# Attention layer: the next image's patches fetched in eight pieces over eight steps, and a third buffer for the result

## The chip, the cores and the metric

The kernel runs on one core of a Trainium2 chip. A core has five instruction queues that run beside each other: TensorE (PE in the profile, with PEld for the loading of its weights), VectorE (DVE), ScalarE (ACT), GpSimd (POOL) and SyncE (SP). They meet only through semaphores. Transfers are carried by 16 DMA engines; an engine's queue issues a transfer and goes on to its next instruction, and whoever needs the data waits for the transfer's semaphore. In this kernel nearly all transfers are issued by SP, one after the other in the order in which they stand in SP's program.

The metric is the device time of one execution in microseconds, as the median of several runs. All arithmetic is in fp32.

## The reference, cut to what matters

The program is four layers on an image batch `x` of shape (8, 16, 256, 256): 8 images, 16 channels, 256 x 256 pixels. Each layer normalises its input by groups of two channels and adds its result to `x`.

```
x = x + L0(gn(x))     # convolution with routing by agreement
x = x + L1(gn(x))     # spline convolution
x = x + L2(gn(x))     # attention over patches: the layer that is changed
x = x + L3(gn(x))     # circular 3x3 convolution
```

The attention layer treats every channel of every image by itself. The 256 x 256 pixels are cut into 16 x 16 patches of 16 x 16 pixels; that is a matrix of 256 patches by 256 pixels.

```
t = (patches + emb).transpose(0, 1, 3, 2)
Q, K, V = t @ Wq.T + bq, t @ Wk.T + bk, t @ Wv.T + bv
A   = sigmoid(einsum('bcph,bcpg->bchg', K, Q) / 16)
out = einsum('bcph,bchg->bcpg', V, A)          # 256 x 256 per image and channel
```

So there are 8 x 16 = 128 independent problems of one size.

## The kernel before

The layers run one after the other. Layer 2, the attention (`layer2`, lines 1432 to 1632), walks through the list `todo`: image by image, and in each image channel by channel, which gives 128 steps. Its instructions stand on every engine in the order in which the Python code issues them: the loop is inside a manual schedule, and no planner moves anything. (The planner with due times at the top of the file belongs to layer 0.)

One step for image b and channel c does the following, in this order:

- In four of 16 steps (c = 2, 6, 10, 14) SP issues the load `res2` (`rows`, line 1480): the layer's input for four channels, in the layout in which it is added to the result. It is 1024 KB, in two buffers that take turns, and the step in which it is issued is two or three steps before its first use.
- At c = 3, `patches` (line 1470) fetches all patches of the next image, in two transfers, one for each half of its 256 patches. Each is issued by `patch` (line 1427): 128 partitions, each with 16 channels x 8 runs of 32 floats (128 B), which is 16,384 runs and 2048 KB. They go to one of two places that take turns by the image's number: image 1, 3, 5, 7 to `pt1`, image 2, 4, 6 to `pt0` (the same memory that layer 3 uses later for its image 0). Image 0 has been fetched at the end of layer 1, by the same function in eight pieces of 512 KB.
- `prepare` for the next step (line 1492): DVE normalises the next channel's patches out of `pt` into `t` (L1496), and POOL adds the embedding and forms four sums (L1500 to L1506).
- `product`, `values`, `rest` (lines 1511 to 1554): PE's matmuls for Q, K and V, and DVE's additions that collect them (L1523 to L1526, L1537 to L1539); ACT turns V into `vt` (L1554).
- `output` for the *previous* step (line 1573): PE multiplies V with A into the PSUM tile `po` (L1579). DVE adds `res2` and writes the result `y2` (L1584), takes its statistics (L1591, L1592); POOL copies the wrapped edge columns (L1593, L1594), and SP issues the store of `y2` to the array `x3` (L1595). One `y2` is 128 partitions x 2064 B, 258 KB.
- `score` (line 1556): PE's product K x Q, and ACT's sigmoid into `a` (L1571), which the next step's `output` reads.

Three orders matter for the change.

- On DVE: L1584 stands behind the current step's L1539 and ahead of the next step's L1496, L1523 and so on. If L1584 waits, all of DVE waits.
- On SP: a step's issues are `res2` if any, then the patches if any, then the store of the previous step's `y2`. That store waits for DVE's L1584 and POOL's copies, so the patches of a step go out right behind the store before.
- Buffers: `y2` has two, so L1584 of one step has to wait until the store of the result two steps earlier has landed. `u2`, `qk` and `a` have one, `t`, `ds`, `vt` and `po` two.

Each transfer on SP also waits until the eighth transfer before it has landed, since eight semaphores take turns.

In the last image (its c from 4 to 12) SP also loads the first two images for layer 3; in that image no patches are fetched, since there is no next image.

Of the kernel before, what the change touches and what calls it, by code (L numbers as in the profile page):

```python
# [10 lines left out]
F32 = mybir.dt.float32  # L11
# [6 lines left out]
B, C, H, W = 8, 16, 256, 256  # L18
P = 128
WP = W + 2  # L20
# [272 lines left out]
class _Net:  # L293
# [1138 lines left out]
    def layer2(self, images=range(B), channels=range(C)):  # L1432
# [3 lines left out]
        with ExitStack() as st:  # L1436
# [3 lines left out]
            mid = st.enter_context(tc.tile_pool(name="l2_mid", bufs=2))  # L1440
# [26 lines left out]

                return get

            def patches(b):  # L1470

                pt = self.pt[b % 2]
                for half in range(2):
                    self.patch(b, half, 0, C)
                return pt

            def rows(b, c):

                res = load.tile([P, 4, 16, 2, 16], F32, name="res2")
                nc.sync.dma_start(  # L1480
                    out=res.rearrange("p c n k j -> p c (n k j)"),
                    in_=self.x2[b][c : c + 4].rearrange("c r h n k j -> (r h) c (n k j)"),
                )
                return res

            pts, ress = {images[0]: self.pt[images[0] % 2]}, {(images[0], 0): first}
# [5 lines left out]
            def prepare(b, c):  # L1492

                bc = final["bc"] if b == images[-1] else self.bc2
                t = self.tpool.tile([P, 2, 8, 32], F32, name="t")
                nc.vector.tensor_scalar(  # L1496
                    t, pts[b][:, :, c], bc[:, 0, b, c : c + 1], bc[:, 1, b, c : c + 1], ALU.subtract, ALU.mult
                )
                t = ts[b, c] = t.rearrange("p h r f -> p h (r f)")
                nc.gpsimd.tensor_tensor(t, t, self.emb0 if c == 0 else emb[:, :, c], ALU.add)  # L1500
                d = sums[b, c] = self.tpool.tile([P, 4, P], F32, name="ds")
                a11, a12, a21, a22 = t[:, 0, :P], t[:, 1, :P], t[:, 0, P:], t[:, 1, P:]
                nc.gpsimd.tensor_tensor(d[:, 0], a21, a22, ALU.add)
                nc.gpsimd.tensor_tensor(d[:, 1], d[:, 0], a11, ALU.subtract)
                nc.gpsimd.tensor_tensor(d[:, 2], a11, a21, ALU.subtract)
                nc.gpsimd.tensor_tensor(d[:, 3], a12, d[:, 1], ALU.subtract)  # L1506
# [4 lines left out]
            def product(b, c):  # L1511

                t, d = ts[b, c], sums[b, c]
                ps = part[b, c] = [psum.tile([P, 256], F32, name=f"pq{i}") for i in range(4)]
                mm(ps[0], t[:, 0, :P], q0, True, True)
                mm(ps[1], d[:, 1], wt[:, 1], True, True)
                mm(ps[2], d[:, 2], wt[:, 2], True, True)
                mm(ps[3], d[:, 0], wt[:, 0], True, True)
                u = mid.tile([P, 2, 256], F32, name="u2", bufs=1)
                qk = qks[b, c] = mid.tile([P, 2, 512], F32, name="qk", bufs=1)  # L1520
                both = bqk.rearrange("p (i n) -> p i n", i=2)
                last = qk[:, 1, 256:]
                nc.vector.tensor_tensor(u, ps[0].unsqueeze(1).to_broadcast([P, 2, 256]), both, ALU.add)  # L1523
                nc.vector.tensor_tensor(u, ps[1].unsqueeze(1).to_broadcast([P, 2, 256]), u, ALU.add)
                nc.vector.tensor_tensor(last, ps[2], u[:, 1], ALU.add)
                nc.vector.tensor_tensor(last, ps[3], last, ALU.add)  # L1526
                part[b, c].append(u)

            def rest(b, c):

                t, d = ts[b, c], sums.pop((b, c))
                *ps, u = part.pop((b, c))
                qk = qks[b, c]
                mm(ps[0], t[:, 1, :P], q1, False, True)
                mm(ps[2], t[:, 1, P:], wt[:, 3], False, True)
                mm(ps[3], d[:, 3], k1, False, True)
                nc.vector.tensor_tensor(qk[:, 0, :256], ps[0], bqk[:, :256], ALU.add)  # L1537
                nc.vector.tensor_tensor(qk[:, 1, :256], ps[2], u[:, 0], ALU.add)
                nc.vector.tensor_tensor(qk[:, 0, 256:], ps[3], u[:, 1], ALU.add)  # L1539

            def values(b, c):

                t = ts[b, c]
                pv = psum.tile([P, 2, 256], F32, name="pv")
                vt = vts[b, c] = mid.tile([P, 2, 2, 8, 2, 8], F32, name="vt")
                for k in range(2):
                    for n in range(2):
                        nc.tensor.matmul(  # L1548
                            pv[:, k], wv[:, n, k * P : (k + 1) * P], t[:, n, :], start=n == 0, stop=n == 1
                        )  # L1550
                for k in range(2):
                    src = pv[:, k].rearrange("p (r i o s) -> p o s i r", r=8, i=2, o=2)
                    for o in range(2):
                        nc.scalar.activation(vt[:, k, o], src[:, o], AF.Identity, bias=bv[:, k : k + 1])  # L1554
# [18 lines left out]
            def output(b, c):  # L1573

                res, vt, a = ress[b, c // 4], vts.pop((b, c)), avs.pop((b, c))
                po = psum.tile([P, 2, 256], F32, name="po", tag="po", bufs=2)
                for o in range(2):
                    for k in range(2):
                        nc.tensor.matmul(  # L1579
                            po[:, o], vt[:, k, o].rearrange("p s i r -> p (s i r)"), a[:, k, :], start=k == 0, stop=k == 1  # L1580
                        )
                y = mid.tile([P, 2, WP], F32, name="y2", bufs=2)
                inner = y[:, :, 1 : 1 + W]
                nc.vector.tensor_tensor(  # L1584
                    inner.rearrange("p o (n j) -> p o n j", j=16),
                    po.rearrange("p o (n j) -> p o n j", j=16),
                    res[:, c % 4].rearrange("p n k j -> p k n j"),
                    ALU.add,
                )
                i = b * C + c  # L1590
                nc.vector.bn_stats(stats[0][:, i, :], inner)  # L1591
                nc.vector.bn_aggr(stats[1][:, :, i], stats[0][:, i])  # L1592
                nc.gpsimd.tensor_copy(y[:, :, 0:1], y[:, :, W : W + 1])  # L1593
                nc.gpsimd.tensor_copy(y[:, :, WP - 1 : WP], y[:, :, 1:2])  # L1594
                nc.sync.dma_start(  # L1595
                    out=self.x3[b][:, c].rearrange("r h k w -> r h (k w)"), in_=y.rearrange("p k w -> p (k w)")
                )

            def step(steps):
                if steps:  # L1600
                    steps.pop(0)[2]()
                while steps and steps[0][0] != "PE":
                    steps.pop(0)[2]()

            with tc.manual_schedule():
                prepare(*todo[0])
                for i, (b, c) in enumerate(todo):
                    n = images.index(b)
                    after = images[n + 1] if n + 1 < len(images) else None
                    if c in (2, 6, 10):  # L1610
                        ress[b, c // 4 + 1] = rows(b, c + 2)
                    if c == 3 and after is not None:
                        pts[after] = patches(after)
                    if c == 14 and after is not None:
                        ress[after, 0] = rows(after, 0)
                    if c == 2 and n == 1:
                        final["bc"], late = self.stats2_steps(self.small, "g2b", bank)
                    if c == 1 and after is None:
                        self.bc3, after3 = self.stats3_steps(self.small, "g3a", bank)
                    if 4 <= c < 13 and after is None:  # L1620
                        self.first3(images[:2], c - 4)
                    if i + 1 < len(todo):
                        prepare(*todo[i + 1])
                    product(b, c)
                    values(b, c)
                    rest(b, c)
                    if i:
                        output(*todo[i - 1])
                    step(late)
                    step(after3)  # L1630
                    score(b, c)
                output(*todo[-1])
# [241 lines left out]
```

## Time and profile before

| | us |
|---|---|
| median of 3 runs | 6216.76 (6212.52 to 6217.24) |
| the profiled execution: its time | 6214.83 |
| the profiled execution: its span, first to last instruction | 6213.1 |
| PE busy in the span | 5875.4 (95%) |
| DVE busy | 5178.3 (83%) |
| POOL busy | 3821.4 (62%) |
| ACT busy | 3074.7 (49%) |
| first result of layer 2 (L1584) starts | 4886.89 |
| last result of layer 2 (L1584) starts | 5981.44 |

The profile is one execution, and every duration in this text is from it. "Busy" is time in which an engine executes; an engine's idle time is listed with whoever released it at its end. The granted clock is the share of PE's full clock that the chip's throttle gave in a stretch. A line number stands for the line of the kernel that issued the instruction. The DMA columns give the mean busy share of the 16 DMA engines and the bytes per second that they moved. For transfers that SP issues the profile has the length of the issue on SP, not the landing; it writes the transfers' sizes in KB of 1024 B, and lists the 14 large patch transfers of layer 2 with a wrong size of 0.1 KB, because their shape is set by a separate instruction (MOVE_SHAPE) ahead of them. The sizes above are counted from line 1427.

### The profile page before, as it was taken

How to read it: one execution, taken by the hardware profiler on the slowest of the kernel's cores; microseconds unless marked ns; L12 is line 12 of the kernel's file. 1: busy time of each engine (PE TensorE's matmuls, PEld its weight loads, DVE VectorE, ACT ScalarE, POOL GpSimd, SP SyncE). 2: the span in 40 equal slices, each digit the busy share in tenths (PEclk: the TensorE clock that was granted, in tenths of full speed). 3: DMA queues.
4: the chain of work that ended last, by engine and by line, in shares of the span. 5: the costliest groups of instructions: out<-in, count | busy, mean ns of one | idle time of the engine just before them, and what ended most of it. 6: DMA issues, size and time to landing. Idle time of an engine off the chain costs nothing.

```text
span 6213.1 us, 114828 instructions
## 1 busy us (share of the span) xinstructions
PE 5875.4 (95%) x45256; PEld 2923.1 (47%) x45256; DVE 5178.3 (83%) x6415; ACT 3074.7 (49%) x4858; POOL 3821.4 (62%) x3552
## 2 busy tenths in 40 slices
PE   2999999999999999999967999999999999999998
PEld 0344444444444444444423444444444688888863
DVE  5799999999999999999978999999999666666641
ACT  0444544454444444444427888888888222121221
POOL 0588888888888888888873334344443334333333
PEclk9999999999999999999978999999999999999999
DMA  7455555455555555555515555555557443444358
GB/s 287 120 138 127 142 142 135 126 145 139 134 130 145 136 133 134 143 138 130 133 45 183 175 176 177 176 173 176 177 176 184 136 84 94 84 98 99 91 179 268
DMA packets 408812, 902.32 MB, mean 145 GB/s; under 512 B 62034, under 2 KB 195762, under 8 KB 364882
## 3 DMA queue, kind: packets, MB, share of 16 engines
q1 hardware_dynamic: 364434, 831.69, 49.0%
q10 hardware_dynamic: 33984, 34.08, 1.8%
q0 software_dynamic: 9856, 29.20, 1.6%
q8 instruction: 359, 5.88, 0.4%
q14 instruction: 179, 1.47, 0.1%
HBM read 684.09 MB, written 210.77 MB: 144 GB/s over the span
## 4 chain that ended last, share of the span: by engine, by line
PE 56%; DVE 27%; issue 7%; DMA 4%; POOL 4%; ACT 2%; DVEq 0%; SPq 0%; POOLq 0%; ACTq 0%
PE rb L831 8%; PE cv L587 7%; DVE bases L1089 7%; PE pq L1509 6%; PE pl L733 6%; DVE e L1079 4%; PE cv L591 4%; PE cv L550 4%; PE po L1579 3%; PE p L1691 3%; PE psc L1563 3%; PE pv L1548 3%; DVE pr L723 2%; DVE a L1079 2%; DVE e L1058 2%
## 5 line engine op out<-in xcount | busy, mean ns | idle before, releaser
L1112 PE MATMUL ps<-bases,tw 128*32 128x512 f32 (+1 forms) x13824 | 1360.9, 545 | 16.2 <-POOL bases L1081 6.6
L851 POOL TENSOR_TENSOR dd<-dd 128x1024 f32<-128x1024 f32 x512 | 1212.7, 2369 | 70.8 <-DVE dd L842 65.5
L1081 POOL TENSOR_TENSOR bases<-e,a 128x1024 f32<-128x1024 f32 (+1 forms) x264 | 621.9, 2379 | 927.4 <-DVE e L1079 927.4
L723 DVE TENSOR_TENSOR pr<-v,fb 128x2048 f32<-128x2048 f32 (+1 forms) x512 | 1021.0, 2015 | 17.0 <-PE pl L733 12.5
L1112 PEld LDWEIGHTS ps<-bases,tw 128*32 128x32 f32 x13824 | 598.5, 109 | 800.1 <-issue 483.8
L842 DVE SCALAR_TENSOR_TENSOR dd<-rb,v 128x1024 f32<-128x1024 f32 x768 | 907.0, 1215 | 8.9 <-POOL dd L851 3.3
L851 POOL TENSOR_TENSOR s<-s,dd 128x512 f32<-128x512 f32 x512 | 648.0, 1276 | 15.1
L831 PE MATMUL rb<-rs,ct_fold 32*128 32x512 f32 x3072 | 593.0, 634 | 25.6 <-DVE pr L723 20.2
L733 PE MATMUL pl<-pr,ct_fold 128*32 128x512 f32 x3584 | 506.9, 603 | 4.3 <-DVE pr L723 4.3
L587 PE MATMUL cv<-kt,w 128*128 128x512 f32 x1024 | 498.0, 609 | 10.8 <-DMA kt<-d 9.6
L851 POOL TENSOR_TENSOR s<-v,dd 128x512 f32<-128x512 f32 x256 | 329.0, 1285 | 290.4 <-DVE dd L842 290.4
L550 PE MATMUL cv<-kt,w 128*128 128x512 f32 x1024 | 476.6, 608 | 5.8 <-DMA kt<-d 5.8
L1089 DVE SCALAR_TENSOR_TENSOR bases<-xr,xm,bases 128x1024 f32<-128x1024 f32 (+1 forms) x264 | 447.1, 1732 | 0.3 <-POOL bases L1081 0.3
L596 ACT COPY v<-cv 128x1024 f32<-128x1024 f32 x256 | 251.9, 1008 | 303.2 <-PE cv L591 303.2
L831 PEld LDWEIGHTS rb<-rs,ct_fold 32*128 32x128 f32 x3072 | 226.2, 185 | 325.5 <-issue 129.3
L1066 ACT ACTIVATE sq<-a 128x1024 f32<-128x1024 f32 (+1 forms) x264 | 263.8, 999 | 231.9 <-DVE a L1058 231.2
L697 PEld LDWEIGHTS fb<-f,ct_fold 64*128 64x128 f32 x3072 | 208.9, 188 | 309.9 <-issue 177.4
L1593 POOL COPY y<-y 128x2 f32<-128x2 f32 x128 | 24.1, 188 | 509.8 <-DVE y L1584 509.8
L842 DVE SCALAR_TENSOR_TENSOR dd<-r,v 128x512 f32<-128x512 f32 x256 | 177.1, 692 | 190.6 <-PE r L831 176.1
L1554 ACT ACTIVATE vt<-pv,w_b2v 128x128 f32<-128x128 f32 x512 | 146.3, 368 | 382.6 <-PE pv L1548 350.2
L1571 ACT ACTIVATE a<-psc 128x512 f32<-128x512 f32 x128 | 76.6, 598 | 514.8 <-PE psc L1563 514.8
L572 ACT COPY v<-cv 128x1024 f32<-128x1024 f32 x256 | 258.1, 1008 | 138.3 <-PE cv L550 138.2
(301 smaller groups left out, 11223.0 us busy)
## 6 DMA issues: line engine op xcount, KB each, us to landing
xr<-x1p SPq DMA_DIRECT2D x120, 1024.0 KB
kt<-d SPq DMA_DIRECT2D x256, 387.0 KB
kt<-d SPq DMA_DIRECT2D x128, 516.0 KB
d<-dn ACTq DMA_DIRECT2D x64, 516.0 KB
kr<-d SPq DMA_DIRECT2D x128, 258.0 KB
kt<-d SPq DMA_DIRECT2D x128, 258.0 KB
x<-y SPq DMA_DIRECT2D x128, 258.0 KB
xs<-in_x_dram SPq DMA_DIRECT2D x16, 2048.0 KB
```

The lines of the kernel that those rows point to most:

```text
L550: nc.tensor.matmul(ps[g]()[:, n], w[:, 0], t[:, a : a + 2, 0:W], start=False, stop=True)
L587: nc.tensor.matmul(ps()[:, n], w2[:, 0, j, :], t[:, a : a + 2, 0:W], start=True, stop=False)
L723: nc.vector.tensor_tensor(pr()[:, :n].rearrange("p n (r w) -> p n r w", w=W), v[h]()[:, 4 * g : 4 * g + n].rearrange("p n (r w) -> p n r w ...
L733: nc.tensor.matmul(pl()[at : at + 32], sel[:, g, h, :], pr()[:, t, :], start=h == 0 and g == 0, stop=h == 1 and (g == 1 or t == 3),)
L831: nc.tensor.matmul(r()[:, n], spread[at, g, h, :], rs()[at], start=True, stop=True)
L842: nc.vector.scalar_tensor_tensor(dd()[:, :n], r()[:, :n], 1.0 / B, v[h]()[:, a : a + n], ALU.subtract, ALU.mult)
L851: op("POOL", us, lambda: nc.gpsimd.tensor_tensor(out[0](), a[0](), b[0](), ALU.add), a[1] + b[1], out[1])
L1079: nc.vector.tensor_tensor(q, q, part[4 + k], ALU.mult)
L1081: nc.gpsimd.tensor_tensor(ring[n % 3][:, 0, p : p + m, 1 : 1 + W], rows(e), rows(a), ALU.subtract)
L1089: nc.vector.scalar_tensor_tensor(r, rows(part[1]), xm[:, b : b + 1], v, ALU.is_gt, ALU.mult)
L1112: nc.tensor.matmul(out if k is None else out[:, k], lhs, rhs, start=start, stop=stop, skip_group_check=True)
L1509: nc.tensor.matmul(out, lhs, rhs, start=start, stop=stop, skip_group_check=True)
```

## The change

The two transfers at c = 3 become eight, one in each of the steps c = 3 to 10. A transfer fetches one half of the patches for four channels: at c = 3 the half 1 of channels 0 to 3, at c = 4 the half 0 of channels 0 to 3, at c = 5 the half 1 of channels 4 to 7, and so on; at c = 10 comes the half 0 of channels 12 to 15. Each is 128 partitions x 32 runs of 128 B: 4096 runs, 512 KB. The bytes, the runs and the destination are the same in sum. The function `patches` is gone. The result `y2` gets three buffers in place of two.

```diff
-            def patches(b):
-
-                pt = self.pt[b % 2]
-                for half in range(2):
-                    self.patch(b, half, 0, C)
-                return pt
...
-                y = mid.tile([P, 2, WP], F32, name="y2", bufs=2)
+                y = mid.tile([P, 2, WP], F32, name="y2", bufs=3)
...
-                    if c == 3 and after is not None:
-                        pts[after] = patches(after)
+                    if 3 <= c < 11 and after is not None:
+                        pts[after] = self.pt[after % 2]
+                        self.patch(after, c % 2, (c - 3) // 2 * 4, 4)
```

In the built program the order of the instructions on PE, DVE, ACT and POOL is the same as before. On SP there are 56 patch transfers in layer 2 in place of 14, each between two stores of `y2`. L1584 (now line 1577) waits for the store three steps earlier in place of two. The third buffer lies behind the other two at the end of the layer's memory, and no other tile has moved.

## The prediction

> **What bounds the kernel now.** First the page's table of 40 slices: layer 2 (4887 to 5982 us) is PE-bound like the rest, but not wholly. Then the timeline of DVE, of which I took the 128 starts of L1584, the result's addition. Their distance is 8.20 us in nearly all steps, and that is PE's pace: the step's own wait, 1.36 us, is for PE's `po`. The exceptions are a few steps with extra normalisation work (8.4 to 12.4 us in images 1 and 7, which stay as they are) and, in every image from 0 to 6, the step c = 4. Here is the one of image 1, where the result before it started at 5048.09:
>
> ```profile
> 5048.09 0.69 DVE L1584 TENSOR_TENSOR y<-po,res 128x512 f32<-128x512 f32 x1 [1.36 <-PE po L1579]
> ...
> 5054.94 0.42 DVE L1539 TENSOR_TENSOR qk<-pq,u 128x256 f32<-128x256 f32 x1
> 5065.80 0.69 DVE L1584 TENSOR_TENSOR y<-po,res 128x512 f32<-128x512 f32 x1 [10.44 <-DMA x<-y]
> ```
>
> It is 17.71 us in place of 8.20, and DVE waited 10.44 us for a store of `y2`. The waits of DVE over layer 2, and PE's, say how often (sum, times, longest):
>
> ```profile
> DVE y L1584 <- PE po L1579: 169.1, 121, 3.1
> ...
> DVE y L1584 <- DMA x<-y: 50.7, 6, 13.1
> ...
> DVE y L1584 <- PE pq L1509: 4.7, 1, 4.7
> ...
> PE pq L1509 <- DVE u L1523: 30.1, 9, 9.4
> ```
>
> Six waits of 50.7 us, and a seventh (image 2) that the profile books on PE although its place and length (4.7 us) are those of the others. PE then waits for DVE. Why the store is late is in SP's timeline of the same stretch:
>
> ```profile
> 5030.54 0.57 SPq L1595 DMA_DIRECT2D x<-y  x1
> 5031.66 15.72 SPq L1427 DMA_DIRECT2D pt<-x  x2
> 5047.49 14.61 SPq L1595 DMA_DIRECT2D x<-y  x1
> ```
>
> SP issues the first 2048 KB of patches at 5031.66, can't get the second out until 5047.4 (an issue is otherwise 0.5 to 0.7 us), and the store behind it until 5062.1. SP's queue takes a new transfer only when most of the one ahead has gone. So the store of the result of 5037.88 is issued some 8 us late and held for 14.6 us more; it lands at about 5065.7, and L1584 needs its buffer. How fast patches flow, in four windows (first two columns: the window and its length; last three: PE's granted clock, DMA share, GB/s):
>
> ```profile
> 4912.00:4920.00 8.00, 8.00 (x39) 7.04 (x38) 5.06 (x11) 1.74 (x5) 3.33 (x7) 1.00 1.18 229
> ...
> 5050.00:5060.00 10.00, 10.00 (x48) 8.81 (x47) 4.00 (x9) 2.34 (x6) 3.01 (x5) 1.00 1.26 146
> 5070.00:5074.00 4.00, 4.00 (x11) 3.24 (x11) 1.51 (x4) 0.00 (x0) 1.18 (x3) 0.54 0.81 296
> 4939.23:4963.84 24.61, 24.61 (x116) 21.66 (x115) 16.53 (x34) 5.22 (x15) 9.98 (x21) 1.00 0.28 76
> ```
>
> 229 GB/s into `pt1` (image 0's fetch), 146 into `pt0` (image 1's), 296 while the load of `res2` runs, and 76 in a quiet stretch, in which the DMA engines are busy 28%. Two rows matter besides: PE's clock is 0.54 after the long stop, so a stop costs more than itself.
>
> **The change part by part.** *What it removes.* The excess of each stop over PE's pace, from the starts of L1584, as the sum of steps 4, 5 and 6 less 3 x 8.20 (so that what PE caught up, and its slow clock afterwards, are inside): image 0: 12.31 + 7.16 + 8.20 - 24.60 = 3.07; image 1: 10.20; image 2: 2.33; image 3: 11.81; image 4: 2.11; image 5: 12.14; image 6: 2.16. Sum 43.82 us, of which 34.15 in the three images that fetch into the slower `pt0`. The chain of waits puts 94 us on the six stores, but PE would have worked through most of that anyway, so that figure is no gain.
>
> *The pieces.* A piece is 512 KB = 524,288 B: 2.3 us at 229 GB/s, 3.6 us at 146. It is issued right behind the store of the step before (258 KB: 1.2 to 1.8 us), and the next store comes 8.20 us after that one. So the queue has 3.5 to 5.4 us of work in a step of 8.20, and the next store finds it free. In c = 6 and c = 10 the 1024 KB of `res2` go ahead of the piece: 4.6 us at 229 to 7.2 us at 146, total 8.1 to 12.6 us. At the worst the store behind is held 4.4 us; the steps after it work 5.4 of 8.2 us, so that this is made up in two steps. I take 0 for it on the path, by the third buffer (next), with 4.4 us x 14 steps as the far end if there were no cover.
>
> *The third buffer.* L1584 needs the store of three results before: it has 3 x 8.20 - 0.69 = 23.9 us where it had 15.7. Needed: about 1 us to the issue, at most 4.4 us held, and a landing of 2.0 to 7.7 us (the range that the profile gives for the tile `y`; those are POOL's stores in layer 3): 13.1 us. Even two buffers would hold that; three leave 10.8 us. Its cost is memory alone.
>
> *SP's issues.* 42 more transfers at 0.7 us (median of line 1427; the eight pieces of layer 1 took 0.47 to 0.93) are 29 us, less 14 MOVE_SHAPE of 0.41 us, which the pieces in layer 1 do not have. What hides it: SP waits for L1584 643.9 us between 5100 and 6100 us. The 1.3 us of a piece and a store in 8.20 us would have to become six times as long to show. The wait for the eighth transfer before lies four steps, some 30 us, back (two to three transfers a step), and binds nothing.
>
> *Who reads the patches.* The first `prepare` of the next image is in step c = 15, five steps (41 us) behind the last piece; before, it was twelve steps. At 12.6 us of queue this is covered. Behind a late piece would stand DVE's L1496 and then all of DVE.
>
> *What is late next.* Nothing in these steps: L1584 again ends on PE's `po` with 1.36 us, as in the 121 others, and PE has no wait. Layer 1 ran with PE 99% busy for 1534 us at a clock of 1.00, so I expect no throttling from the smoother load.
>
> The Trainium skill ("DMA: Bandwidth & Descriptors", Rules for kernel authors and the anatomy of one DMA) speaks against small transfers: it advises 1 MiB or more, and puts about 2 us on each transfer whatever its size. By that page 42 more transfers would be an estimated 84 us, if they lay on the path one after the other. No row here shows two pieces without other work between them; nothing in the sum uses this.
>
> *Sum.* The profiled execution's own time is 6214.83 (span 6213.1); 6214.83 - 43.82 = 6171.0. It stands 1.93 below the median of the runs, so 6172.9 against that: **6173**.
>
> **The rivals.**
> 1. *The pieces are slow one by one, and SP becomes the bound (the other side).* In layer 1 the store behind a piece sat on SP for 6.9 to 9.7 us (issues of L1160 behind L1427). If a piece by itself held the queue for 9.7 us, a step with one would take SP 0.6 + 0.6 + 9.7 = 10.9 us against 8.20: 2.7 x 56 = 151 us, and the time 6173 + 151 = 6324. It decides from 7.0 us a piece on. Against it: in layer 1 each of those steps had some 2 MB of other loads ahead of the piece, at 166 to 205 GB/s, which accounts for 10 us and more; and one transfer of four times the bytes held the queue for 14.7 us here, 3.7 us a quarter. The Trainium skill's fixed 2 us (same page) would belong here, and with 3.6 us would not reach 7.0.
> 2. *Part of the stop stays,* at the two steps with `res2` of the images that fill `pt0`: 3 x 2 x 4.4 = 26 us, time 6199. It needs the store to be 24 us late, against the 13.1 above.
> 3. *The change doesn't do it:* the stores are held for another reason than the patches, the waits stay, 6217. Against it: all seven stops are at c = 4, right behind the only step with patches, and SP's blocked issues lie there alone.
>
> **How the numbers follow.** Forecast 0.86 (6167 to 6181: the runs' spread of 2 to 4 us, and up to half of the 14 steps leaving 1 us); rival 2: 0.05; rival 3: 0.03; rival 1: 0.06. The measurement tells 0.2%, 12 us, from no change: faster 0.91, same 0.03, slower 0.06. The range reaches from 6167 towards rival 2, to 6188.
>
> **What would show it.** L1584 (now L1577) starts 8.20 us apart in c = 3 to 11 of images 0 to 6; DVE's wait for the store of `y` is gone from the list of waits; SP's issues of line 1427 number 56 in layer 2, each below 1 us, with no store issue over 3 us except behind `res2`; the clock is 1.00 in images 1, 3 and 5, where 0.96 to 0.98 stood. Wrong it is if stores show issues of 7 us and more in every step (rival 1), if L1584 waits for the store at c = 7 to 9 or 11 to 13 (rival 2), or if L1496 waits for the patches.

## The result, and the profile after

| | before | after |
|---|---|---|
| median of the runs, us | 6216.25 (6212.52 to 6217.24, 4 runs) | 6174.08 (6168.51 to 6176.98, 4 runs) |
| ratio, 95% interval | | 0.9932 [0.992, 0.9944] |
| span of the profiled execution, us | 6213.1 | 6166.7 |
| layer 2, from its first to its last start of the result's addition, us | 1094.55 | 1050.93 |

The change takes 42.2 us off the median, 0.7%; 6173 was forecast. Of the 46.4 us between the two spans, layer 2 has 43.6. Another 3.2 lie ahead of it (its first addition starts at 4883.72 in place of 4886.89), and 0.4 are lost behind it; both parts are unchanged code and scatter by more than this between executions. For that reason the experiments below are compared by the length of layer 2 first.

A step of DVE is named here, as in the prediction, by the channel whose result it writes. The loop writes the result of channel c while it works on channel c + 1, so the patches that the loop issues at c = 3 stand in SP's queue ahead of the stores of the results 2 and 3, and it is the result 4 that needs the buffer of the result 2.

The step c = 4 of image 1, in DVE's timeline after (the line numbers are seven lower now):

```profile
5048.63 0.42 DVE L1532 TENSOR_TENSOR qk<-pq,u 128x256 f32<-128x256 f32 x1
5050.35 0.69 DVE L1577 TENSOR_TENSOR y<-po,res 128x512 f32<-128x512 f32 x1 [1.30 <-PE po L1572]
```

The addition comes 8.63 us after the one before (5041.72) and waits for PE alone. DVE's waits and PE's over layer 2 (sum, times, longest):

```profile
DVE y L1577 <- PE po L1572: 167.2, 127, 3.1
...
DVE y L1577 <- DMA pt<-x: 1.3, 1, 1.3
...
PE pq L1502 <- DVE qk L1518: 1.3, 2, 0.6
...
PE pq L1502 <- DVE u L1516: 0.6, 2, 0.4
```

No wait for a store of `y2` is left, and PE's 30.1 us of waiting for DVE's L1523 have become 0.6 (now L1516). The one wait of 1.3 us that ended on a transfer lies in image 7, where it replaces a wait for PE of the same length: the step takes 8.43 us, before 8.42. SP's timeline around c = 6 of the loop in image 3, one of the steps with `res2`:

```profile
5313.90 0.58 SPq L1588 DMA_DIRECT2D x<-y  x1
5314.53 0.45 SPq L1473 DMA_DIRECT2D res<-x  x1
5315.04 0.70 SPq L1427 DMA_DIRECT2D pt<-x  x1
5322.10 1.01 SPq L1588 DMA_DIRECT2D x<-y  x1
5323.15 0.46 SPq L1427 DMA_DIRECT2D pt<-x  x1
```

The store behind `res2` and a piece sits on SP for 1.01 us where 0.58 is usual. The longest issue of a store in all of layer 2 is 1.93 us; it was 14.61. The 56 issues of line 1427 take 0.36 to 0.72 us. Windows of three stretches (columns: window, length, busy time of PE, PEld, DVE, ACT and POOL, PE's granted clock, DMA share, GB/s):

```profile
5160.00:5300.00 140.00, 140.00 (x650) 123.25 (x649) 94.22 (x188) 29.61 (x85) 57.00 (x121) 1.00 0.47 97
...
5570.00:5710.00 140.00, 140.00 (x651) 123.23 (x650) 94.27 (x188) 29.61 (x85) 57.07 (x120) 1.00 0.49 97
4939.23:4963.84 24.61, 24.61 (x116) 21.66 (x115) 16.53 (x34) 5.23 (x16) 9.98 (x21) 1.00 0.61 124
```

PE is busy for all of the 140 us, at its full clock. The stretch 4939 to 4964, quiet before with 28% of the DMA engines, has 61% now: the patches have moved into it.

### The profile page after: what moved, and what is told of

Same layout as the page of the kernel before. It is cut to its first block, busy times and chain, and to the rows that moved or that the text cites. A ratio compares the mean times of both kernels' runs of the same rounds, so it can differ in the third digit from the quotient of the medians.

```text
span 6166.7 us, 114828 instructions
## 1 busy us (share of the span) xinstructions
PE 5863.3 (95%) x45256; PEld 2919.8 (47%) x45256; DVE 5179.4 (84%) x6415; ACT 3074.9 (50%) x4858; POOL 3820.8 (62%) x3552
## 2 busy tenths in 40 slices
DMA packets 581515, 902.32 MB, mean 146 GB/s; under 512 B 292082, under 2 KB 368466, under 8 KB 537586
## 4 chain that ended last, share of the span: by engine, by line
PE 58%; DVE 27%; issue 7%; POOL 3%; DMA 3%; ACT 2%; SPq 0%; DVEq 0%; POOLq 0%; ACTq 0%
PE rb L831 8%; PE cv L587 7%; DVE bases L1089 7%; PE pq L1502 6%; PE pl L733 6%; DVE e L1079 4%; PE cv L591 4%; PE cv L550 4%; PE po L1572 4%; PE psc L1556 4%; PE pv L1541 4%; PE p L1685 3%; DVE pr L723 2%; DVE a L1079 2%; DVE a L1058 2%
## 5 line engine op out<-in xcount | busy, mean ns | idle before, releaser
L831 PE MATMUL rb<-rs,ct_fold 32*128 32x512 f32 x3072 | 594.3, 636 | 25.6 <-DVE pr L723 20.1
L1048 ACT ACTIVATE d<-xr,bd,sd 128x1024 f32<-128x1024 f32 (+1 forms) x264 | 319.0, 1208 | 14.0 <-DMA xr<-x1p 13.9
L550 PEld LDWEIGHTS cv<-kt,w 128*128 128x128 f32 x1024 | 184.5, 190 | 290.0 <-issue 281.7
```

The costliest lines, as they stand in the source:

```text
L550: nc.tensor.matmul(ps[g]()[:, n], w[:, 0], t[:, a : a + 2, 0:W], start=False, stop=True)
L831: nc.tensor.matmul(r()[:, n], spread[at, g, h, :], rs()[at], start=True, stop=True)
```

## The experiments

| run | median, us | ratio to before [95%] | layer 2, us |
|---|---|---|---|
| before | 6214.3 to 6222.49 | | 1094.55 |
| after | 6174.08 | 0.9932 [0.992, 0.9944] | 1050.93 |
| eight pieces, two buffers | 6174.29 | 0.9921 [0.9905, 0.9938] | 1051.17 |
| two transfers at c = 3, three buffers | 6182.54 | 0.9937 [0.9922, 0.9952] | 1053.93 |
| eight pieces, all at c = 3 | 6225.13 | 1.0009 [0.9999, 1.0018] | 1101.26 |
| one half at c = 3, one at c = 7 | 6175.03 | 0.9928 [0.9913, 0.9943] | 1051.17 |
| `pt0` moved to a multiple of 128 B | 6189.5 | 0.9958 [0.9944, 0.9973] | 1061.06 |
| two pieces a step, c = 3 to 6 | 6176.72 | 0.9939 [0.9924, 0.9954] | 1051.17 |
| two stores issued by ACT | 6170.8 | 0.9929 [0.9913, 0.9946] | 1053.55 |
| `pt1` moved off the multiple | 6262.02 (one run, before 6217.19) | | 1133.13 |
| `pt0` at 32 B off the multiple | 6237.25 (one run, before 6217.19) | | 1096.58 |

The runs of the kernel before beside each group had medians of 6216.25, 6222.49, 6214.3 and 6217.19 us; each ratio is to its own group's. The lengths of layer 2 are from one profiled execution each. They contain up to 1.7 us that vary without a change: in image 7 the step c = 2 takes 10.7 us in some executions and 12.4 in others.

### Which of the two parts does it

First the pieces without the third buffer, and then the buffer without the pieces.

```diff
-                y = mid.tile([P, 2, WP], F32, name="y2", bufs=3)
+                y = mid.tile([P, 2, WP], F32, name="y2", bufs=2)
```

> Eight pieces in eight steps, but two buffers for the result. Theory A (the stop came from the stores being held behind 4 MB of patches in SP's queue): a store is held at most 1.9 us now and lands some 8 us after its result, against 15.7 us that two buffers allow, so no stop is left: layer 2 lasts as long as in the changed kernel (1051 us), time 6170 to 6177. Rival B (the third buffer is what removes the stop): waits of L1577 for a store come back in the steps c = 5 to 12, some 2 us in each of the two steps behind a load of res2, time 6185 to 6200.

Measured: 6174.29 us, layer 2 1051.17 us, no wait for a store, longest store issue 1.70 us. Rival B falls: the third buffer adds nothing to the pieces.

```diff
-                y = mid.tile([P, 2, WP], F32, name="y2", bufs=2)
+                y = mid.tile([P, 2, WP], F32, name="y2", bufs=3)
```

(in the kernel before)

> Two transfers of 2 MB at c = 3 as before, but three buffers for the result. By theory A the store is held as long as before; what changes is who needs it: c = 4 finds a free buffer, and c = 5 needs the store that landed 34 us after the fetch began in image 1. Worked out from the landings before: c = 5 would come 1.2, 3.0 and 3.6 us before the landing in images 1, 3 and 5, and not at all in the others. Some 5 us of the 43.8 stay: time 6173 to 6180, layer 2 1052 to 1058 us. If the fetch itself slowed the steps (another cause than the buffers), the stops would stay: 6216.

Measured: layer 2 1053.93 us, as expected; the time, 6182.54, lies 2.5 us above what was written, beside runs of the kernel before that were 6 us above the first ones (the ratio is 0.9937). DVE's waits in layer 2 of this run:

```profile
DVE y L1584 <- PE po L1579: 163.3, 124, 3.1
...
DVE y L1584 <- DMA x<-y: 11.9, 3, 4.7
```

The wait for a store is still there, in three steps (c = 5 of images 1, 3 and 5). They cost 0.34, 2.08 and 2.26 us, taken from the steps c = 5 and 6 less 2 x 8.20: 4.7 us of the 43.8, where some 5 were worked out. The store itself is as late as before (an issue of up to 14.02 us); only the one who needs it comes later. So the third buffer alone takes away nine tenths of the stops, and the pieces alone all of them.

### Size or place in time

```diff
-                for half in range(2):
-                    self.patch(b, half, 0, C)
+                for k in range(8):
+                    self.patch(b, (k + 1) % 2, k // 2 * 4, 4)
                 return pt
```

(in the kernel before: eight pieces, all at c = 3)

> Eight pieces of 512 KB, all issued at c = 3, two buffers: the size of the after kernel at the place of the before kernel. Theory A with the rates of the large transfers (146 and 229 GB/s): the same stop as before, 6212 to 6220. Theory A with the rate that a piece shows in the changed kernel's trace (its last part alone moves at 107 to 109 GB/s, and its packets are of 128 B where the large transfers had 512 B): 4 MB take 39 us into either place, L1584 is some 17 to 19 us late in every image, time 6280 to 6305. Rival C (only large transfers hold SP's queue, small ones do not): no stop, 6171 to 6177.

Measured: 6225.13 us beside 6222.49 of the kernel before, layer 2 1101.26. All seven stops are back. Rival C falls, and of the two sums of theory A the one with 39 us for every fetch falls too: pieces in a row do not move at 107 to 109 GB/s. The first sum holds beside the kernel before (ratio 1.0009); the time itself lies 5 us above what was written, where the runs before lay 6 us above the first ones. SP's timeline at image 1, and two windows:

```profile
5030.07 0.57 SPq L1595 DMA_DIRECT2D x<-y  x1
5030.70 26.65 SPq L1427 DMA_DIRECT2D pt<-x  x8
5057.46 8.85 SPq L1595 DMA_DIRECT2D x<-y  x3
```

```profile
4908.00:4916.00 8.00, 8.00 (x39) 7.04 (x38) 5.51 (x11) 1.74 (x5) 3.32 (x7) 1.00 1.26 198
5044.00:5054.00 10.00, 9.49 (x43) 8.17 (x44) 6.92 (x15) 1.43 (x5) 5.04 (x11) 1.00 1.65 145
```

The eight issues keep SP for 26.65 us, and the store behind them goes out from 5057.46 on, some 19 us after its result is ready (L1584 starts at 5037.40). Into `pt0` (second window) eight pieces flow at 145 GB/s, like two large transfers (146); into `pt1` at 198 in place of 229, which makes the stops of images 0, 2, 4 and 6 18.65 us in sum where they were 9.67.

```diff
-                    if c == 3 and after is not None:
-                        pts[after] = patches(after)
+                    if c in (3, 7) and after is not None:
+                        pts[after] = self.pt[after % 2]
+                        self.patch(after, c // 4, 0, C)
```

(in the kernel before: whole halves, four steps apart)

> The two transfers of 2 MB stay whole, but one goes at c = 3 and one at c = 7; two buffers. Theory A: one half holds the queue 9 to 14.7 us, so the store behind it is issued up to 7 us late and lands some 13 us after its result, against 15.7: no stop, time 6170 to 6178. Rival C: 14 large transfers, 14 stops; if each costs half of what the pair cost, 6205 to 6217.

Measured: 6175.03 us, layer 2 1051.17 us, DVE's waits without a store. A store still sits on SP for up to 9.86 us behind a half, but two buffers cover that. It isn't the size of a transfer that mattered, but the 4 MB between two stores.

```diff
-                    if 3 <= c < 11 and after is not None:
+                    if 3 <= c < 7 and after is not None:
                         pts[after] = self.pt[after % 2]
-                        self.patch(after, c % 2, (c - 3) // 2 * 4, 4)
+                        for half in range(2):
+                            self.patch(after, half, (c - 3) * 4, 4)
...
-                y = mid.tile([P, 2, WP], F32, name="y2", bufs=3)
+                y = mid.tile([P, 2, WP], F32, name="y2", bufs=2)
```

(in the kernel after: two pieces a step, two buffers)

> Two pieces in each of the four steps c = 3 to 6, two buffers for the result. At the rates that eight pieces in a row showed (195 GB/s into pt1, 145 into pt0) a step has 6.6 to 9.0 us of transfers in 8.20, and c = 6 with its res2 up to 16 us; the store behind c = 6 is held some 8 to 10 us and lands 13 to 15.5 us after its result, against 15.7. Theory A: still no stop, or below 1 us in images 1, 3 and 5: 6171 to 6180. If a piece cost more by itself than its bytes (the skill's fixed time, rival 1 of the prediction), SP falls behind by more than 2 us in each of the four steps and L1577 waits for a store in the steps c = 7 to 9: 6190 and more.

Measured: 6176.72 us, layer 2 1051.17 us. SP sits up to 7.53 us on the second piece of a pair, but it is free again for the store: the longest store issue is 3.08 us, where 8 to 10 were worked out behind `res2`. Even at twice the density the fetch leaves no stop, so the prediction's rival 1 was far off.

### The queue, or the DMA engines

```diff
-                nc.sync.dma_start(
+                queue = nc.scalar if c in (2, 3) and b != images[-1] else nc.sync
+                queue.dma_start(
                     out=self.x3[b][:, c].rearrange("r h k w -> r h (k w)"), in_=y.rearrange("p k w -> p (k w)")
                 )
```

(in the kernel before)

> The kernel before (both transfers of 2 MB at c = 3, two buffers), but the stores of the results c = 2 and c = 3 of images 0 to 6 are issued by ACT, which has a queue of its own. Theory A as the prediction has it (the store is late because it stands behind the patches in SP's queue): it is issued within 1.5 us of its result, takes its share of the DMA engines beside the patches, and lands within 10 us: no stop, layer 2 1051 to 1054 us, time 6171 to 6182. Rival D (the 16 DMA engines are full, whoever issues): the store lands only when the 4 MB have gone, as before: 1090 us and more, 6212 to 6220.

Measured: 6170.8 us, layer 2 1053.55 us, no wait for a store. SP's timeline of image 1, and ACT's:

```profile
5025.98 15.84 SPq L1427 DMA_DIRECT2D pt<-x  x2
5054.80 3.21 SPq L1596 DMA_DIRECT2D x<-y  x1
```

```profile
5033.29 0.58 ACTq L1596 DMA_DIRECT2D x<-y  x1
5033.90 1.28 ACT L1292 ACT_TABLE_LOAD   x1 [3.65 <-POOL y L1594]
...
5046.16 0.60 ACTq L1596 DMA_DIRECT2D x<-y  x1
```

The patches keep SP until 5041.8, for as long as before, but the store is issued at 5033.29 on ACT's queue, and its buffer is free in time. When its bytes moved is in the DMA queues (q1 is SP's, q10 ACT's; packets, MB, and the packets' time as a share of 16 engines), first from 5033 to 5041 us, then from 5041 to 5045:

```profile
q1 hardware_dynamic: 2248, 1.15, 120.4%
...
q1 hardware_dynamic: 776, 0.39, 69.2%
q10 hardware_dynamic: 136, 0.26, 19.7%
```

For nearly 8 us after its issue nothing of ACT's store moves. By 5045 all of it has moved, with the end of the first 2 MB and some 15 us before the end of the second. So rival D as it was put falls: the store does not wait for the 4 MB. But it did not take its share beside the patches either, as the expectation had it: it waited for the transfer that was under way, and was spared the one that stands ahead of it in SP's queue. It landed 12 us after the start of its addition (5032.19), where 10 were expected. Why it waited, no run shows. SP's own stores behind the second 2 MB are still held, for up to 7.80 us, which two buffers cover. The 2.6 us that layer 2 has more than the changed kernel are in one step, c = 3 of image 1 (12.88 us in place of 10.15): there ACT's normalisation work stands behind the store, which waits for POOL's copies (the wait of 3.65 us above).

### Why images 1, 3 and 5 stopped for longer

The prediction took 146 and 229 GB/s from the trace without a reason. `pt0` starts 32192 B into each partition, 64 B off a multiple of 128, and `pt1` at 123264, on one.

```diff
+        pool.tile([P, 16], F32, name="gap0")
         self.x30 = pool.tile([P, 33 * WP], F32, name="pt0")
+        pool.tile([P, 16], F32, name="gap1")
```

(in the kernel before)

> The kernel before, with pt0 moved by 64 B inside every partition (32192 to 32256, so that its start is a multiple of 128 B like that of pt1, 123264 before and 123392 now); all that follows moves by 128 B. Nothing else differs. If the 146 GB/s into pt0, against 229 into pt1, come from where the runs of 128 B begin in memory, the stops of images 1, 3 and 5 shrink to those of the others (2 to 3 us each): layer 2 lasts 1094.6 - 27 = 1067 us, time some 6190 against 6217. If they come from the source or from the image, nothing changes: 6212 to 6222.

Measured: 6189.5 us, layer 2 1061.06 us; the steps c = 4 and 5 of images 3 and 5 take 11.47 + 7.53 and 10.80 + 7.16 us, where they took 19.43 + 9.13 and 19.97 + 8.57. The fetch into `pt0` now flows like that into `pt1`:

```profile
5034.00:5040.00 6.00, 6.00 (x31) 5.31 (x30) 2.68 (x10) 3.60 (x5) 0.31 (x2) 1.00 1.17 225
5046.00:5050.00 4.00, 4.00 (x21) 3.51 (x20) 3.63 (x7) 0.60 (x1) 1.77 (x4) 1.00 1.21 221
```

Some three quarters of what the change gains in layer 2 (33.5 of 43.6 us, 1.7 of them image 7's scatter) could have been had by 64 B of padding ahead of `pt0`; in the medians of the runs it is 24.8 us beside the change's 42.2. The counter-test moves `pt1` off:

```diff
+            one.tile([P, 16], F32, name="gap0")
             self.pt.append(one.tile([P, 2, C, 8, 32], F32, name="pt1"))
+            one.tile([P, 16], F32, name="gap1")
```

(in the kernel before)

> The kernel before, with pt1 moved by 64 B inside every partition (123264, a multiple of 128, to 123328, which is not; pt0 stays at 32192, all that follows moves by 128 B). If a start off the multiple of 128 B is what slows the fetch, the stops of images 0, 2, 4 and 6 grow from 2 to 3 us to the 10 to 12 us of images 1, 3 and 5, the windows show 146 GB/s into pt1 too, and layer 2 lasts some 1094.6 + 33 = 1128 us. If the earlier run on pt0 was about something else (the place relative to other tiles), 1095 us.

Measured, from one execution: layer 2 1133.13 us; the step c = 4 takes 19.8 to 20.1 us in images 0, 2, 4 and 6 (11.3 to 12.3 before), and both halves of image 0's fetch show

```profile
4904.00:4912.00 8.00, 8.00 (x39) 7.04 (x38) 5.31 (x12) 1.74 (x5) 3.12 (x7) 1.00 1.21 146
4916.00:4924.00 8.00, 8.00 (x39) 7.04 (x38) 1.27 (x3) 1.74 (x5) 0.61 (x2) 1.00 1.24 146
```

And `pt0` once more, 32 B further than the multiple:

```diff
+        pool.tile([P, 24], F32, name="gap0")
         self.x30 = pool.tile([P, 33 * WP], F32, name="pt0")
+        pool.tile([P, 8], F32, name="gap1")
```

(in the kernel before)

> As the run that moved pt0 to a multiple of 128 B (32256), but 32 B further, at 32288. If any start off the multiple of 128 B makes the fetch slow, images 1, 3 and 5 stop for 10 to 12 us again, with 146 GB/s or less: layer 2 1094 us. If only a start of 64 B off is slow: 1061 us.

Measured, from one execution: layer 2 1096.58 us, with the stops of images 1, 3 and 5 back (17.59, 19.90 and 20.10 us for c = 4) and 145 to 147 GB/s. So 32 and 64 B off are equally slow. This execution's 6237.25 us are 20 us above the kernel before although layer 2 is only 2 us longer; the rest is 5 us ahead of layer 2 and 15 behind it. It is not explained: the part behind layer 2 lasted from 231 to 247 us in the profiled executions of this study, 246 among them in the run with eight pieces and two buffers, where `pt0` had not been moved.

## Why the prediction was right

*The stop and what it costs.* Right in place, cause and size. The sum of the excesses was 43.82 us, layer 2 lost 43.62. 0.43 us of the excess was wrongly in the sum: the step c = 4 of image 1 takes 8.63 us without any stop, since it follows the normalisation work of that image. That 6173 and 6174.08 lie 1 us apart is partly luck: the runs of the changed kernel alone spread over 8.5 us. That the chain of waits put 94 us on the stores and only 44 were to be had is borne out.

*That the stores stood behind the patches in SP's queue.* Right, and shown by the two stores issued by ACT while SP was still held. The first of them was spared the second 2 MB, while each of the two had to wait for the 2 MB that were under way. The rule that SP's queue takes a new transfer only when most of the one ahead has gone holds for patches behind patches, and not for a piece behind `res2`, which goes out in 0.70 us (5315.04 above).

*The pieces.* The term of the sum that was mis-sized. The prediction gave a store and a piece 3.5 to 5.4 us, by the rates of transfers that stand in a row. Windows of the changed kernel around one store and one piece (image 0):

```profile
4902.00:4904.00 2.00, 2.00 (x11) 1.76 (x10) 1.70 (x4) 0.50 (x1) 1.59 (x2) 1.00 0.65 72
4904.00:4906.00 2.00, 2.00 (x11) 1.75 (x10) 0.99 (x3) 0.70 (x3) 1.42 (x4) 1.00 1.09 226
4906.00:4908.00 2.00, 2.00 (x11) 1.77 (x10) 1.00 (x3) 0.44 (x2) 0.00 (x0) 1.00 0.61 98
4908.00:4910.00 2.00, 2.00 (x11) 1.77 (x10) 1.61 (x4) 0.00 (x0) 0.31 (x2) 1.00 0.02 3
```

It is some 6 us: the transfer starts and ends slowly, and reaches 226 GB/s only in the middle. From the store's issue to the piece's last packet it is 7.0 us on average, in the packets of the trace and in the steps without `res2`. The margin in a step of 8.20 us was 1 to 2 us and not 2.8 to 4.7. Since nothing waits for the queue's end, that had no price. Nor does the place count here, where the prediction took 2.3 us for a piece into `pt1` and 3.6 into `pt0`. The second and the third of these windows, as far behind a store of image 1 whose piece goes into `pt0`:

```profile
5070.64:5072.64 2.00, 2.00 (x11) 1.75 (x10) 0.99 (x3) 0.70 (x3) 1.42 (x4) 1.00 1.09 228
5072.64:5074.64 2.00, 2.00 (x11) 1.77 (x10) 1.00 (x3) 0.44 (x2) 0.00 (x0) 1.00 0.60 94
```

From the store's issue to the last packet it is 7.1 us into `pt0`. A lone piece is as fast into either place, so that in the changed kernel the slow place costs nothing. From the end of such a piece (107 to 109 GB/s) I worked out, for the eight pieces at c = 3, far too long a stop: the rate at the end of a transfer is not the rate of a stream.

*`res2` ahead of a piece.* Held 1.35 us at most (an issue of 1.93 less the usual 0.58); the bound was 4.4. From the store's issue to the piece's last packet it is 9.2 us into either place, where 8.1 to 12.6 were worked out. Right in sign, and covered.

*The third buffer.* "Even two buffers would hold that" is borne out by the pieces with two buffers.

*SP's issues.* 0.46 us each at the median, 0.7 was taken; hidden in any case. L1489 never waits for the patches, and PE's clock is 1.00, as said.

*The rivals.* Rival 1 (a piece holds the queue 7 us and more by itself) is excluded by two pieces a step, and rivals 2 and 3 by the list of waits. The Trainium skill ("DMA: Bandwidth & Descriptors", Anatomy of one DMA, SWDGE (gpsimd) path) was weighed with its 2 us for each transfer, which that section gives for transfers that GpSimd issues; the patches are issued by SP. 56 transfers and 14 give layer 2 the same length to 0.01 us (pieces with two buffers, and halves apart), since nobody waits for their landing. In a row, by the packets in the traces, eight into `pt1` took 24.7 us from the first issue to the last packet and two took 23.2 (means of four fetches each), some 0.3 us for each one more; into `pt0` both took 31.5. The 2 us themselves no run here shows.

## What to carry to other kernels

A store that frees a buffer shares its queue with bulk loads: look for it behind them, and put no more between two stores than the buffers allow; space the loads, add a buffer or use another queue, since each of the three took away nine tenths of the stops or more here. Another queue spares a store the transfers that are still to be issued, but here not the one under way. Take the worth of a stop from the rhythm of the steps around it, not from the chain's share or the length of the wait. Before reordering slow transfers, compare their rate with that of the same transfer into another place, and look at where in the partition that place begins.

## What was not expected of the hardware

- In transfers of 2 MB, runs of 128 B written to an SBUF place that starts on a multiple of 128 B flow at 221 to 229 GB/s, and at 145 to 147 if it starts 32 or 64 B off, while the DMA engines show much the same busy share (1.17 to 1.26; the share adds up the times of packets that overlap, so it can pass 1). Three runs with nothing but padding in the diff show it in both directions. Eight pieces in a row differ too (198 and 145), lone pieces do not (7.0 and 7.1 us). The Trainium skill ("DMA: Bandwidth & Descriptors", How a descriptor splits into AXI transactions) counts in boundaries of 256 B. An estimate by its table for single runs of 128 B gives 6 beats of 32 B on average on the multiple of 128, 8 at 64 B off and 7 at 32 B off; the measured ratio is 1.57 for 64 and the same for 32. The table speaks of reads, and these are writes; what sets the rate is not settled here.
- SP's queue holds little more than one transfer of patches: right behind 2 MB an issue of SP takes 9.5 to 15.5 us, right behind another piece (eight in a row) 2.4 to 5.1 us, and 7 us behind a piece 0.58. It is not the bytes alone that fill it: `res2` with 1024 KB and a piece behind it go out in 0.45 and 0.70 us. `res2` is 512 runs of 2048 B, a piece 4096 runs of 128 B; whether the number of runs decides was not tested.
- A store issued on ACT's queue while 2 MB from SP's queue are under way moves only towards their end: its first packet starts 4.2 to 8.8 us after its issue in the seven images (8.45 in image 1).
- The same runs of 128 B are moved as packets of 512 B in the transfers of 2 MB and of 128 B in the pieces: the page counts 62,034 packets under 512 B before and 292,082 after, 230,048 more for 56 x 4096 = 229,376 runs. Eight pieces in a row flow as fast as two transfers into `pt0` and an eighth slower into `pt1`; whether that comes from the packets or from the number of transfers was not tested.
